# The list products of stage one moved into the slots of the masks

## The chip, the cores and the metric

The kernel runs on one core of a Trainium2 chip. The metric is the device time of one execution in microseconds; several executions are measured and their median is given. Five engines work side by side, each through its own instructions in order: TensorE (PE in the profile, with its weight loads as PEld), VectorE (DVE), ScalarE (ACT), GpSimd (POOL) and SyncE (SP), which here only starts DMAs. Engines wait for each other through semaphores.

## The reference

One layer on 4096 nodes with 512 features: attention over a sparse adjacency matrix, then a mixture of experts.

```python
x = x + gnn(layernorm(x), adj)
#   q, k, v = x @ Wq[h], x @ Wk[h], x @ Wv[h]            8 heads of 64
#   scores = q k^T / 8 + 0.01 eye - 1e16 (1 - max(adj, eye))
#   out = sum over h of softmax(scores) v @ Wo[h]
x = x + ffn(layernorm(x))
#   logits = x @ Wg + bg; the two best of 8 experts, softmax of their logits as weights
#   y_e = gelu(x @ W1[e] + b1[e]) @ W2[e] + b2[e]
```

The adjacency matrix is random and thin, denser for the first nodes than for the last.

## The kernel before, in words

Rows are handled in 32 tiles of 128 nodes, and eight groups of four tiles. The kernel has a stage one (projections and lists), a stage two (attention over lists of needed keys, with the routing of the experts beside it) and a stage for the experts. If a list has no room, a general path runs afterwards; it isn't used with this data.

**Stage one** (lines 322 to 623) does two things at once.

- *Projections.* For each of the 32 tiles x is normalised (`stats`, `norm` on VectorE), turned on TensorE (`turn_x`, two halves) and multiplied with the weights of k, v and, one block of four tiles later, q. Each product has four parts of 128 x 512 (lines 589 and 604). ScalarE copies the sums out of PSUM, and ScalarE's queue stores them to DRAM (`kv_d`, `q_d`).
- *Lists.* The adjacency matrix is loaded in 64 pieces, each of four row tiles by 512 columns, into seven buffers (`load_a`). `masks` (line 478) multiplies a piece with a small matrix `pw` of 32 columns, once for each of the four tiles, each into its own 32 partitions; so the array works in tiles of 128 rows by 32 columns. The result packs 16 rows into a number, and tells whether a column has an edge in the upper or lower half of a tile. ScalarE copies it, `turn_masks` turns it back on TensorE (line 492), ScalarE casts the words (line 496), and VectorE makes the indicators `ind` (line 497). When eight pieces of a group are done, `places` works out which list position each needed key gets: `classes`, `number` (two small products, lines 180 and 183), `ranks`, `outer`, `slots`, all else on VectorE. `group_lists` then builds the lists. `rows` and `values` fill `r_all` (lines 268, 277), one buffer that all groups share. `hot` (line 281) builds one of 16 one-hot matrices, in five buffers. `quads` (line 294) multiplies one of them: eight small products, 128 rows by 32 columns, into the four quarters of one PSUM tile; two `quads` make the sixteen that the profile shows together. `copy` takes the sum to SBUF on ScalarE, and `keys` turns it (line 308) and makes the indices `idx` on VectorE (lines 310 to 315).

The order is written out by hand. The function `job(n, f)` puts a piece of work into slot n; `step()` issues the work of the next slot in the order in which it was put there, and one part of a projection (two instructions of TensorE) follows it. There are 384 slots: eight for each of the first four tiles, twelve for each other, sixteen at the end. `masks(h)` stands in slot 5 + 5h, its turning three slots later. With s the slot behind the last mask of a group by five (s = 45 + 40g for group g), `places` takes the slots s, s+1, s+2, s+5 and s+8, and the jobs of `group_lists` follow. The masks of the following groups stand at s, s+5, s+10 and so on up to slot 320, so jobs of neighbouring groups are interleaved.

**Stage two** starts by closing the buffers of stage one. One large tile, `ring`, takes the place of most of them; SP loads a tile's own rows and its q (lines 691, 709), and POOL gathers the keys and values of the lists into it (line 696). TensorE turns the keys (line 723), ScalarE copies them (`kT`, line 725), and scores (line 760), exponentials (line 767), masks (line 773) and value products (line 788) follow.

Of the kernel before, what the change touches and what calls it, by code (L numbers as in the profile page):

```python
# [70 lines left out]
def fast(tc, dram, flag, x, adj, Wks, Wqs, Wvs, Wo, Wg, bg, W1, b1, W2, b2, out):  # L71
    with ExitStack() as ctx:
        _fast(ctx, tc, dram, flag, x, adj, Wks, Wqs, Wvs, Wo, Wg, bg, W1, b1, W2, b2, out)


def _fast(ctx, tc, dram, flag, x, adj, Wks, Wqs, Wvs, Wo, Wg, bg, W1, b1, W2, b2, out):
# [248 lines left out]
    with ExitStack() as s1:  # L325
# [198 lines left out]
        def job(n, f, *args):  # L524
            jobs.setdefault(n, []).append(lambda: f(*args))

        begins = [0]
        for i in range(NT):
            begins.append(begins[-1] + (2 * DC if i < TPB else 3 * DC))
            s = begins[i]  # L530
# [7 lines left out]
        for h in range(NHC):  # L538
            s = 5 + 5 * h
            job(s, masks, h)  # L540
            job(s + 1, load_a, h + 7)
            job(s + 3, turn_masks, h)
            g, c = divmod(h, NH)
            if c == NH - 1:
                s += 5
                hold = {}

                def ready(g=g, hold=hold):
                    hold["p"] = places(g, inds[g], lp, ps_l, "l")
                    hold["l"] = group_lists(g, rp, ohp, ps_l, "l")  # L550

                def call(hold, k, n, *args):
                    hold[k][n](*args)

                job(s, ready)
                for d, n in ((0, 0), (1, 1), (2, 2), (5, 3), (8, 4)):
                    job(s + d, call, hold, "p", n)
                job(s + 9, call, hold, "l", 0)
                job(s + 10, call, hold, "l", 1)
                for x2 in range(NT // 2):  # L560
                    job(s + 11 + 2 * x2, call, hold, "l", 2, x2)
                    job(s + 16 + x2 // 2 * 4, call, hold, "l", 3, x2)
                job(s + 44, call, hold, "l", 4)
                job(s + 47, call, hold, "l", 5)

        def extras():
            nc.scalar.dma_start(out=wg, in_=Wg.rearrange("(c p) e -> p c e", p=P))
# [1425 lines left out]
```

## Time and profile before

| | us |
|---|---|
| median of 3 runs | 2074.48 (2071.14 to 2076.76) |
| the profiled execution | 2230.39 |
| its span | 2228.6 |
| stage one: first and last projection product | 7.6 to 465.56 |
| TensorE busy, whole span | 2003.9 (90%) |
| VectorE busy, whole span | 959.3 (43%) |
| ScalarE busy, whole span | 790.9 (35%) |
| list products, line 294 | 1024 instructions, 26.9 busy |
| mask products, line 478 | 256 instructions, 26.1 busy |
| projection products, lines 589 and 604 | 768 instructions, 387.6 busy |

A line of the profile gives the source line, the engine, the operation, what is written and read with sizes, and how often. In the order of time, the first two numbers are the start and the time that the line covers, and the bracket tells how long the engine was idle before and what released it. In the table of stretches, each engine's busy time stands with its number of instructions, followed by the granted TensorE clock, the share of the DMA engines' time and GB/s. In the list of waits, the numbers are the total time, how often, and the longest. The profiled execution is longer than the runs without a profile.

### The profile page before, as it was taken

How to read it: one execution, taken by the hardware profiler on the slowest of the kernel's cores; microseconds unless marked ns; L12 is line 12 of the kernel's file. 1: busy time of each engine (PE TensorE's matmuls, PEld its weight loads, DVE VectorE, ACT ScalarE, POOL GpSimd, SP SyncE). 2: the span in 40 equal slices, each digit the busy share in tenths (PEclk: the TensorE clock that was granted, in tenths of full speed). 3: DMA queues.
4: the chain of work that ended last, by engine and by line, in shares of the span. 5: the costliest groups of instructions: out<-in, count | busy, mean ns of one | idle time of the engine just before them, and what ended most of it. 6: DMA issues, size and time to landing. Idle time of an engine off the chain costs nothing. (4 is left out here: it accounts for less than half of the span.)

```text
span 2228.6 us, 59742 instructions
## 1 busy us (share of the span) xinstructions
PE 2003.9 (90%) x25491; PEld 1329.7 (60%) x25491; DVE 959.3 (43%) x2501; ACT 790.9 (35%) x1152; POOL 611.7 (27%) x721
## 2 busy tenths in 40 slices
PE   9899999979999879888969697887967999999996
PEld 4344444459887757767858586776754444444443
DVE  3455655525444434534535344443554333333332
ACT  3232333235554534534535253443421222222221
POOL 2000000054444345433243443324122222222221
PEclk9999999989999979989989798998978999999998
DMA  9778775287777568767576575766686455565542
GB/s 371 253 251 257 255 246 179 77 350 252 246 259 257 201 228 266 249 206 239 190 267 232 202 255 204 255 201 222 227 278 195 104 115 113 111 144 111 110 72 44
DMA packets 193411, 462.01 MB, mean 207 GB/s; under 512 B 30384, under 2 KB 46768, under 8 KB 193008
## 3 DMA queue, kind: packets, MB, share of 16 engines
q0 software_dynamic: 67024, 249.44, 36.8%
q1 hardware_dynamic: 101808, 177.51, 24.8%
q10 hardware_dynamic: 24304, 31.11, 4.0%
q8 instruction: 206, 3.38, 0.6%
q14 instruction: 69, 0.57, 0.1%
HBM read 385.37 MB, written 72.64 MB: 206 GB/s over the span
## 5 line engine op out<-in xcount | busy, mean ns | idle before, releaser
L696 POOL DMA_INDIRECT ring<-kv_d,idx x361 | 407.3, 1128 | 978.1 <-ACT l L303 438.0
L760 PE MATMUL ps<-q,kT 64*64 64x64 f32 (+1 forms) x10224 | 356.5, 242 | 112.4 <-issue 96.0
L773 DVE SCALAR_TENSOR_TENSOR pr<-t,pr 128x1024 f32<-128x1024 uint16 x238 | 284.9, 1226 | 369.8 <-ACT pr L767 367.4
L760 PEld LDWEIGHTS ps<-q,kT 64*64 64x64 f32 (+1 forms) x10224 | 304.3, 151 | 166.1 <-issue 135.9
L788 PE MATMUL o<-ring,pr 128*64 128x65 f32 x8640 | 308.9, 228 | 31.6 <-issue 31.3
L725 ACT COPY kT<-pkT 128x512 f32<-128x512 f32 (+1 forms) x270 | 198.8, 783 | 375.5 <-PE pkT L723 268.6
L767 ACT ACTIVATE pr<-ps 128x1024 f32<-128x1024 f32 x270 | 271.4, 1025 | 139.4 <-PE ps L760 104.0
L788 PEld LDWEIGHTS o<-ring,pr 128*64 128x64 f32 x8640 | 282.1, 141 | 52.3 <-issue 37.5
L1341 PE MATMUL ph<-ring,xT 128*128 (+1 forms) x528 | 238.2, 594 | 0.8 <-ACT xT L1303 0.8
L723 PE MATMUL pkT<-ident,ring 128*128 128x128 f32 x1572 | 211.3, 282 | 18.3 <-issue 16.7
L723 PEld LDWEIGHTS pkT<-ident,ring 128*128 128x128 f32 x1572 | 180.0, 145 | 46.3 <-issue 38.7
L1392 POOL DMA_INDIRECT out_dram<-y,r x66 | 101.8, 1542 | 366.2 <-ACT y L1387 266.8
L1370 PE MATMUL py_e<-ring,hT 128*128 (+1 forms) x396 | 182.3, 596 | 1.6 <-ACT hT L1363 1.6
L1341 PEld LDWEIGHTS ph<-ring,xT 128*128 128x128 f32 (+1 forms) x528 | 91.3, 183 | 99.8 <-issue 98.7
L1387 ACT ACTIVATE y<-y,wt 128x512 f32<-128x512 f32 x66 | 47.6, 722 | 269.6 <-DVE y L1383 229.8
L604 PE MATMUL pv<-wv,xT 128*128 128x512 f32 x256 | 131.3, 608 | 0.0
L604 PE MATMUL pk<-wk,xT 128*128 128x512 f32 x256 | 130.4, 621 | 0.7 <-ACT xT L399 0.7
L589 PE MATMUL pq<-xT,wq 128*128 128x512 f32 x256 | 125.9, 607 | 0.0
L1029 POOL DMA_INDIRECT xs_d<-x,slot_i x64 | 64.6, 1010 | 203.2 <-DVE t L735 90.2
L828 PE MATMUL py<-wo,oT 128*128 128x512 f32 x256 | 119.3, 609 | 0.7 <-ACT oT L822 0.7
L1346 DVE COPY h<-ph 128x512 f32<-128x512 f32 x66 | 45.6, 692 | 169.6 <-PE ph L1341 166.1
L1370 PEld LDWEIGHTS py_e<-ring,hT 128*128 128x128 f32 (+1 forms) x396 | 67.2, 183 | 76.0 <-issue 74.1
(293 smaller groups left out, 1893.7 us busy)
## 6 DMA issues: line engine op xcount, KB each, us to landing
adj<-in_adj_dram SPq DMA_DIRECT2D x64, 1024.0 KB
wo<-in_L_ffn_W_dram SPq DMA_DIRECT2D x72, 256.0 KB
kv_d<-kvr ACTq DMA_DIRECT2D x32, 516.0 KB
ring<-kv_d SPq DMA_DIRECT2D x32, 516.0 KB
r<-xs_d SPq DMA_DIRECT2D x57, 258.0 KB
ring<-in_L_ffn_W_dram SPq DMA_DIRECT2D x56, 256.0 KB
xt<-in_x_dram SPq DMA_DIRECT2D x32, 256.0 KB
q_d<-qT ACTq DMA_DIRECT2D x32, 256.0 KB
```

The source lines that it names most:

```text
L589: nc.tensor.matmul(pq, w["q"][:, c, ts(p, P)], xTs[b][:, c, :], start=(c == 0), stop=(c == DC - 1),)
L604: nc.tensor.matmul(pk, xTs[b][:, c, ts(t, P)], w[n][:, c, :], start=(c == 0), stop=(c == DC - 1),)
L696: nc.gpsimd.indirect_dma_start(out=g, out_offset=None, in_=kv_d, in_offset=bass.IndirectOffsetOnAxis(ap=idx[i // GL][:, i % GL, a : a + 1] ...
L723: nc.tensor.transpose(pk[:, x * NP + p, :], g[:, ts(p, P)], ident)
L725: nc.scalar.copy(kT[:, : nk * NP], pk[:, : nk * NP])
L760: nc.tensor.matmul(ps[c : c + nk, r, p * P + x * nq : p * P + (x + 1) * nq], kT[r * KD : (r + 1) * KD, p, c : c + nk], q[r * KD : (r + 1) ...
L767: nc.scalar.activation(pr.rearrange("p h q -> p (h q)"), ps.rearrange("p r f -> p (r f)"), AF.Exp)
L773: nc.vector.scalar_tensor_tensor(pr, st["t"].unsqueeze(1).to_broadcast([P, H, P]), 0.0, pr, op0=ALU.is_gt, op1=ALU.mult,)
L788: nc.tensor.matmul(o[c * HALF : (c + 1) * HALF, h // NP, (h % NP) * VW : (h % NP + 1) * VW], pr[:, hd * NP + p, c * HALF : (c + 1) * HALF] ...
L828: nc.tensor.matmul(hold["py"], hold["oT"][:, c, :], wo[:, c, :], start=(c == 0), stop=(c == NP - 1),)
L1341: nc.tensor.matmul(ph[a], xTs[b][:, c, a], w, start=(c == 0), stop=(c == DC - 1), skip_group_check=b >= FULL,)
L1370: nc.tensor.matmul(py[a], hTs[b][:, c, a], w, start=(c == 0), stop=(c == HC - 1), skip_group_check=b >= FULL,)
```

## The change

The jobs of `group_lists` get other slots. `rows` and `values` move one slot back, from s+9 and s+10 to s+10 and s+11. The one-hot matrices were built every second slot from s+11; now two are built in every five slots, at s+10, s+12, s+15, s+17 and so on to s+47. The products of two one-hot matrices stood together every fourth slot from s+16 to s+44; now they stand every fifth slot from s+15 to s+50, which are the slots of the following groups' masks. `copy` and `keys` go from s+44 and s+47 to s+52 and s+55. `places` and the masks keep their slots. Within a slot, a group's list jobs are put in before the masks of the groups behind it.

```diff
                 for d, n in ((0, 0), (1, 1), (2, 2), (5, 3), (8, 4)):
                     job(s + d, call, hold, "p", n)
-                job(s + 9, call, hold, "l", 0)
-                job(s + 10, call, hold, "l", 1)
+                job(s + 10, call, hold, "l", 0)
+                job(s + 11, call, hold, "l", 1)
                 for x2 in range(NT // 2):
-                    job(s + 11 + 2 * x2, call, hold, "l", 2, x2)
-                    job(s + 16 + x2 // 2 * 4, call, hold, "l", 3, x2)
-                job(s + 44, call, hold, "l", 4)
-                job(s + 47, call, hold, "l", 5)
+                    m = 5 * (x2 // 2)
+                    job(s + 10 + m + 2 * (x2 % 2), call, hold, "l", 2, x2)
+                    job(s + 15 + m, call, hold, "l", 3, x2)
+                job(s + 52, call, hold, "l", 4)
+                job(s + 55, call, hold, "l", 5)
```

The numbers behind "l" are the places in the list that `group_lists` returns: 0 `rows`, 1 `values`, 2 `hot`, 3 `quads`, 4 `copy`, 5 `keys`.

## The prediction

> **What bounds the kernel now.** I read the page first, then the busy time by stretch, then the costliest groups of the first 470 us, the waits, and last the order of time. Slots are those of the code: one slot is one `step()` and the projection product behind it, 384 in all, slot 0 near 7.6 us, the last product ending at 465.56. Busy time of PE, PEld, DVE, ACT, POOL by stretch:
>
> ```profile
> 100.00:150.00 50.00, 50.00 (x299) 22.71 (x300) 28.90 (x86) 16.43 (x36) 0.00 (x0) 1.00 0.74 246
> 150.00:200.00 50.00, 50.00 (x309) 22.21 (x307) 27.55 (x83) 16.10 (x37) 0.00 (x0) 1.00 0.78 252
> 250.00:300.00 50.00, 50.00 (x309) 22.79 (x297) 27.25 (x84) 16.26 (x36) 0.00 (x0) 1.00 0.76 254
> ```
>
> In stage one TensorE has no free moment at full clock (1.00), VectorE is busy 55%, the DMA engines 0.74 to 0.78. Stage one ends when TensorE ends, so time taken out of TensorE's stream is won, unless VectorE becomes late. From the waits of this stretch:
>
> ```profile
> DVE oh L281 <- PE list L294: 12.7, 5, 2.9
> PEld L294 <- DVE oh L281: 3.0, 4, 0.8
> PEld L478 <- DMA adj<-in_adj_dram: 2.3, 3, 0.8
> ```
>
> The mask products wait little for the adjacency loads (2.3 us in all). The second line is the weight loader's idle time; whether the list products are delayed is seen in the order of time, which also gives the prices (start, us, engine):
>
> ```profile
> 156.05 1.02 PE L604 MATMUL pk<-wk,xT 128*128 128x512 f32 x2
> 157.00 0.42 PE L294 MATMUL list<-oh,r_all 128*32 128x128 f16 x16
> 157.35 1.13 PE L604 MATMUL pk<-wk,xT 128*128 128x512 f32 x2
> 158.31 0.60 PE L492 MATMUL pwt<-ident,ws 128*128 128x128 f32 x4
> 158.75 1.88 PE L604 MATMUL pk<-wk,xT 128*128 128x512 f32 x4
> 160.56 0.41 PE L478 MATMUL pwd<-adj,pw 128*32 128x512 bf16 x4
> 160.90 1.13 PE L604 MATMUL pv<-wv,xT 128*128 128x512 f32 x2
> ...
> 165.87 1.02 PE L589 MATMUL pq<-xT,wq 128*128 128x512 f32 x2
> 166.82 0.42 PE L294 MATMUL list<-oh,r_all 128*32 128x128 f16 x16
> 167.06 0.41 PE L478 MATMUL pwd<-adj,pw 128*32 128x512 bf16 x4
> 167.40 1.13 PE L589 MATMUL pq<-xT,wq 128*128 128x512 f32 x2
> ```
>
> A projection product is two instructions, 0.429 us from start to start (1.88 us for four is three such steps and 0.59). List products alone: 157.35 - 156.05 = 1.30, less 2 x 0.429 = 0.44, and the product behind them starts its second half 0.11 late (1.13 against 1.02): 0.55 us. Mask products alone: 160.90 - 158.75 = 2.15, less 4 x 0.429 = 0.43, plus 0.11: 0.54. Both in one slot: 167.40 - 165.87 = 1.53, less 0.86, plus 0.11: 0.78. I took the same difference over all of stage one: 31 list products alone 0.543 to 0.552, 44 mask products alone 0.535 to 0.538, 9 pairs 0.770 to 0.785. So a pair costs 0.547 + 0.537 - 0.777 = 0.307 us less than its two parts, and no list product is late now (none above 0.552).
>
> **What the skill says.** The Trainium skill, "TensorEngine Tiling (Array Packing)", Key Properties: "Changing tiling mode (not just tile) drains the TensorE". The trace agrees: in front of each such stretch the step is 0.52 instead of 0.43, and behind it the next weights are loaded in the open (0.11). "TensorE: Matmul & The Clock Gate", Part 2, says that weight loads are pulled ahead of running matmuls; the table shows that this is lost at a change. "Perfetto Trace Analysis", Tensor Engine Instruction: TensorE's ends are modelled, and VectorE and ScalarE run strictly in order. So I use starts, and treat VectorE as a queue.
>
> **The change part by part.** Nothing is added or removed: each group still has 16 `hot`, 16 `quads`, and one each of `rows`, `values`, `copy`, `keys`. No DMA is issued by a moved job.
>
> *Pairs.* Group g ends at s = 45 + 40g, and masks stand at multiples of 5, the last at slot 320. Before, quads stand at s+16, 20, 24 ... 44, so only s+20 and s+40 meet a mask: 13 pairs (two each for g = 0 to 5, one for g = 6). After, they stand at s+15, 20 ... 50: eight pairs each for g = 0 to 5, five for g = 6, none for g = 7: 53. In such a slot quads come first and masks directly behind, as in the 13. That is 40 new pairs x 0.307 = 12.3 us won. Lost: seven list products stood beside a mask's turning, which saved 0.04 to 0.05 each: 0.3. Net 12.0.
>
> *VectorE's order.* Before, a group's last two one-hots (s+39, s+41) are built ahead of the next group's `ranks`; after, they stand at s+45 and s+47, behind `ranks` and between it, `outer` and `slots`. In exchange `keys` leaves that place (s+47 to s+55). From the order of time around 166 to 187: `ranks` takes 168.72 to 172.34 = 3.62, `outer` 173.87 to 177.03 = 3.16, `slots` 178.96 to 180.74 = 1.78, a one-hot 0.61, statistics 0.84, normalising 0.65, an `ind` 0.1. With t = 0 at the first scan, one-hot 15 ends at 3.62 + 0.1 + 0.61 + 3.16 + 0.84 + 0.61 + 0.13 = 9.1; 9.7 where normalising stands there too. TensorE reaches its quads (s+50) after N 0.33, nine slots 7.72, two turnings 0.88, a pair 0.78 and one or two halves of x's turning 0.2 to 0.4, less 0.36 from N's start to the scan: 9.6 to 9.8. The margin, about 2 us or more before, is half a microsecond to nothing.
>
> *The wait that is new.* `rows` of the next group (s+50) overwrites `r_all`, which quads 14 and 15 of the same slot read; before, five slots lay between. Behind it on VectorE are values and the first one-hots, for which the quads of s+55 wait. But VectorE comes to `rows` only at about 9.1 + 1.78 + 0.75 = 11.6, and TensorE has left those quads by 10.1, so it costs nothing; if VectorE were early it would wait, harmlessly, for 1.5 us. From 11.6, rows, values (0.99 and 0.88 at twelve columns) and two one-hots end at 14.8; TensorE comes to s+55 at 9.7 + 0.78 + 4.29 + 0.44 + 0.2 = 15.4. For group 0 `rows` and `values` take 2.0 each; its one-hots are ready 1.7 us ahead now and its quads move 1.4 earlier (a slot and a mask). Going through all groups so, with the trace's durations and each engine in order, I get delays of 0.4 in three groups: 1.2 us. That walk, made for the order of before, hits the traced start of each VectorE block to 0.3 us where stage one runs undisturbed. Bounds: 0 and 1.5 us per group, 10.5.
>
> *The end of stage one.* The ring of stage two lies where `r_all` and the one-hots lay, so its first loads wait for the last quads:
>
> ```profile
> 451.96 0.42 PE L294 MATMUL list<-oh,r_all 128*32 128x128 f16 x16
> 452.43 0.63 SPq L709 DMA_DIRECT2D q<-q_d  x1
> 453.29 1.07 POOL L696 DMA_INDIRECT ring<-kv_d,idx  x1 [438.02 <-ACT l L303]
> ...
> 473.56 0.29 DVE L735 TENSOR_TENSOR t<-own_words,bits 128x128 uint16<-128x128 uint16 x1 [16.71 <-DMA q_d<-qT]
> 473.82 0.59 ACT L725 COPY kT<-pkT 128x512 f32<-128x512 f32 x1 [6.90 <-issue]
> ```
>
> These quads move from slot 369 to 375, six slots or 5.15 us nearer the end; SP's queue (q, own rows) and POOL's gathers start that much later against the end. The page names the copy of the list (slot 369, then 377), which is eight slots, 6.9. What hides it: stage two can't go on before 473.8, when the last q_d store, issued at 466.95, has landed. By the trace's landings gather 1 is there at 460.6, gathers 2 and 3 at 465.0, gather 4 at 466.5; TensorE needs them at 467, 468 and 474.5. Moved by 5 to 7 us, only 2 and 3 are late for their first use, and the store still sets the end. Later turns (483, 490) use gathers that landed 11 us and more before. I take 0; the other end is 5.2 us of loss where the cover is gone; a gain of 1.5 us is possible, since fewer gathers stand beside that store. The last keys (slot 380) are used near the end of stage two.
>
> **Sum.** 12.3 - 0.3 - 1.2 - 0 = 10.8 us off the profiled 2230.39 us (span 2228.6, 1.8 around it). The median of the runs shown, 2074.48, is 156 us lower; stage one's products already run at full clock, so I take the 10.8 unscaled: 2063.7 us, 0.5% faster. About 0.3% (6.2 us) is what a measurement can tell from no change.
>
> **Rivals.**
> - VectorE as the wait in place of the drain: 0.9 to 1.6 us of delay in each of seven groups eats 6 to 11 of the 12.0: 2069 to 2074, taken at 2072. For: margins near zero. Against: VectorE idles for 3 to 4 us between two `ind` in mid-group and catches up. Chance 0.13.
> - Stage two starts later: the 5.2 us not hidden: 2069. For: gathers keep the DMA engines full from 453. Against: the 473.8 above. Chance 0.10, half of it below the bound.
> - The adjacency loads are the limit and TensorE waits for them instead: 2074. Against: seven buffers and 0.76 of DMA time. Also here: the change does nothing, the pair's price holding only in the places seen. Chance 0.05.
> - Slower: the same VectorE queue between s+41 and s+55, but late by more than 12.0 / 7 = 1.7 us in each group, the point from which it decides. That needs 2 us more work or waiting in 15 us than the traced durations give, say where ScalarE holds `ind` behind a statistics wait in every group. At 3 us: 7 x 3 - 12 = 9 slower, 2083. Chance 0.06.
>
> **How the numbers follow.** Likeliest, 0.66: 2063.7, own range 2061 to 2067. Faster by over 0.3%: 0.66, half of the second rival and 0.06 of the first: 0.77. Same: 0.17. Slower: 0.06. The range runs from 2059.5 (no delays, 1.5 won at the stage's change, and the runs' scatter) to 2071, which takes in the second rival and part of the first and leaves out under 0.2.
>
> **What would show it.** Right: 53 pairs at 0.78 and 11 list products alone; the last projection product near 454.8 instead of 465.6; list products late by under 0.5 us, at x2 = 15 and x2 = 0 alone; first gather near 447.5; kT at 8 us behind the last product. Wrong: waits of list products for the one-hots of over 1 us in most groups; pairs above 0.9; more than 9 us from the last product to kT.

## The result and the profile after

| | before | after |
|---|---|---|
| median of the timed runs, us | 2074.48 (2071.14 to 2076.76) | 2068.03 (2065.06 to 2070.81) |
| ratio, 95% interval | | 0.9973 [0.9960, 0.9986] |
| stage one, from the start of the first product to 0.43 behind the start of the last, us | 457.85 | 447.83 |
| list and mask products sharing a stretch | 13 | 53 |
| list products alone | 51 | 11 |
| mask products alone | 51 | 11 |

The kernel became 6.45 us faster, 0.31% by the medians and 0.27% by the ratio of the runs, so just about what the prediction called measurable; 2063.7 was forecast, with a range to 2071. Stage one became 10.0 us shorter in the two profiled executions. So about 3.6 us of what was won in stage one did not arrive at the end.

One thing has to be known to read the profiles. The kernel before takes about 2223 us on two chips used below and 2074.77 on a third. By its time the profile of before (2230.39 us) comes from a chip like the first two; behind the end of stage one it is about 150 us longer than the profile of after (2070.29 us), which comes from one like the third, as the timed runs do. It is not the profiling that makes it longer: each profiled execution of the other kernels lies within the range of that kernel's timed runs (after: 2065.06 to 2070.81). So stage one is compared between these two profiles, stage two is not. For stage two the same kernels were run side by side on one chip, below.

Stretches of stage one in the kernel after; per engine the busy time and the number of instructions, then clock, DMA share and GB/s:

```profile
100.00:150.00 50.00, 50.00 (x319) 23.64 (x318) 29.25 (x86) 17.05 (x38) 0.00 (x0) 1.00 0.76 252
150.00:200.00 50.00, 49.88 (x318) 23.41 (x317) 29.56 (x88) 16.83 (x38) 0.00 (x0) 1.00 0.79 270
250.00:300.00 50.00, 50.00 (x321) 23.91 (x320) 29.41 (x88) 17.07 (x38) 0.00 (x0) 1.00 0.80 269
```

TensorE is as full as before and gets more done: 319, 318 and 321 instructions against 299, 309 and 309 in the same 50 us. VectorE rises with it to 58 or 59%, and the DMA engines to 0.76 to 0.80; neither has become the limit. The order of time on TensorE in the kernel after (start, us, instruction):

```profile
152.47 0.42 PE L294 MATMUL list<-oh,r_all 128*32 128x128 f16 x16
152.72 0.40 PE L478 MATMUL pwd<-adj,pw 128*32 128x512 bf16 x4
153.05 1.13 PE L590 MATMUL pq<-xT,wq 128*128 128x512 f32 x2
...
157.98 0.42 PE L294 MATMUL list<-oh,r_all 128*32 128x128 f16 x16
158.23 0.40 PE L478 MATMUL pwd<-adj,pw 128*32 128x512 bf16 x4
158.56 1.12 PE L605 MATMUL pv<-wv,xT 128*128 128x512 f32 x2
...
163.93 0.42 PE L294 MATMUL list<-oh,r_all 128*32 128x128 f16 x16
164.17 0.40 PE L478 MATMUL pwd<-adj,pw 128*32 128x512 bf16 x4
164.50 1.12 PE L590 MATMUL pq<-xT,wq 128*128 128x512 f32 x2
```

Lines behind line 565 have moved by one (L590 was L589). In these lines every list product has the mask product 0.24 or 0.25 us behind it, and one long product step (1.12 or 1.13 instead of 1.02) behind both: the open weight load is paid once. Read as in the prediction, the 39 plain pairs cost 0.775 us (median), 8 pairs with a turning of x beside them 0.997 (that turning alone costs 0.221), and 6 with the turning of a list 0.887 (0.112 alone). The waits of the kernel after (total, how often, longest):

```profile
DVE oh L281 <- PE list L294: 15.4, 5, 4.0
PEld L478 <- DMA adj<-in_adj_dram: 1.5, 2, 0.8
PE list L294 <- DVE oh L281: 0.7, 2, 0.4
PEld L294 <- DVE oh L281: 0.5, 1, 0.5
```

The mask products wait even less for the adjacency loads (1.5 us against 2.3). The last two lines are where TensorE waits for one-hots: the late list products of the prediction. The largest loss is at 223 us: the last list products of group 2, whose one-hots stand behind the places of group 3 on VectorE (L224 to L249). The second half of the stretch is 0.42 us late:

```profile
222.91 0.29 DVE L232 TENSOR_TENSOR place<-place,part 128x128 f32<-128x128 f32 x1
223.12 0.69 DVE L281 TENSOR_TENSOR oh<-sp,count 128x1024 f16<-128x1024 f16 x1
223.13 0.30 PE L294 MATMUL list<-oh,r_all 128*32 128x128 f16 x8
223.85 0.30 PE L294 MATMUL list<-oh,r_all 128*32 128x128 f16 x8 [0.42 <-DVE oh L281]
```

And the change of stage:

```profile
446.45 0.42 PE L294 MATMUL list<-oh,r_all 128*32 128x128 f16 x16
446.91 0.64 SPq L710 DMA_DIRECT2D q<-q_d  x1
447.77 1.07 POOL L697 DMA_INDIRECT ring<-kv_d,idx  x1 [432.46 <-PE list L294]
...
458.55 0.66 PE L724 MATMUL pkT<-ident,ring 128*128 128x128 f32 x4 [1.85 <-DMA ring<-kv_d,idx]
...
462.64 0.29 DVE L736 TENSOR_TENSOR t<-own_words,bits 128x128 uint16<-128x128 uint16 x1 [9.79 <-DMA q_d<-qT]
462.81 2.48 ACT L726 COPY kT<-pkT 128x512 f32<-128x512 f32 x4 [7.27 <-DMA q_d<-qT]
```

Stage one ends at 454.74. The last list product is 8.1 us ahead of that (13.2 before) and the first gather 7.0 (12.1 before). TensorE now waits for a gather at 458.55, but `kT` still waits for the store of q and starts 8.1 us behind the end, as it did before (8.4).

### The profile page after: what moved, and what is told of

The parts are those of the page before. It is cut to its first block, busy times and chain, and to the rows that moved or that the text cites. A ratio compares the mean times of both kernels' runs of the same rounds, so it can differ in the third digit from the quotient of the medians.

```text
span 2068.6 us, 59754 instructions
## 1 busy us (share of the span) xinstructions
PE 1927.7 (93%) x25491; PEld 1287.7 (62%) x25491; DVE 957.1 (46%) x2501; ACT 790.9 (38%) x1152; POOL 605.1 (29%) x721
## 5 line engine op out<-in xcount | busy, mean ns | idle before, releaser
L697 POOL DMA_INDIRECT ring<-kv_d,idx x361 | 395.5, 1096 | 840.7 <-PE list L294 432.5
L789 PE MATMUL o<-ring,pr 128*64 128x65 f32 x8640 | 297.5, 225 | 44.2 <-issue 44.0
L761 PE MATMUL ps<-q,kT 64*64 64x64 f32 (+1 forms) x10224 | 306.6, 237 | 31.1 <-issue 23.3
L761 PEld LDWEIGHTS ps<-q,kT 64*64 64x64 f32 (+1 forms) x10224 | 272.6, 148 | 64.1 <-issue 44.0
L789 PEld LDWEIGHTS o<-ring,pr 128*64 128x64 f32 x8640 | 273.1, 139 | 62.6 <-issue 47.3
L724 PE MATMUL pkT<-ident,ring 128*128 128x128 f32 x1572 | 204.7, 279 | 8.0 <-DMA ring<-kv_d,idx 2.8
L1342 PEld LDWEIGHTS ph<-ring,xT 128*128 128x128 f32 (+1 forms) x528 | 91.3, 183 | 99.8 <-issue 98.7
L605 PE MATMUL pk<-wk,xT 128*128 128x512 f32 x256 | 125.7, 610 | 0.7 <-ACT xT L399 0.7
L1030 POOL DMA_INDIRECT xs_d<-x,slot_i x64 | 69.8, 1090 | 186.1 <-DVE t L736 89.1
L590 PE MATMUL pq<-xT,wq 128*128 128x512 f32 x256 | 123.1, 603 | 0.0
```

Source lines behind the costliest of these rows:

```text
L590: nc.tensor.matmul(pq, w["q"][:, c, ts(p, P)], xTs[b][:, c, :], start=(c == 0), stop=(c == DC - 1),)
L605: nc.tensor.matmul(pk, xTs[b][:, c, ts(t, P)], w[n][:, c, :], start=(c == 0), stop=(c == DC - 1),)
L697: nc.gpsimd.indirect_dma_start(out=g, out_offset=None, in_=kv_d, in_offset=bass.IndirectOffsetOnAxis(ap=idx[i // GL][:, i % GL, a : a + 1] ...
L724: nc.tensor.transpose(pk[:, x * NP + p, :], g[:, ts(p, P)], ident)
L761: nc.tensor.matmul(ps[c : c + nk, r, p * P + x * nq : p * P + (x + 1) * nq], kT[r * KD : (r + 1) * KD, p, c : c + nk], q[r * KD : (r + 1) ...
L789: nc.tensor.matmul(o[c * HALF : (c + 1) * HALF, h // NP, (h % NP) * VW : (h % NP + 1) * VW], pr[:, hd * NP + p, c * HALF : (c + 1) * HALF] ...
```

## The experiments

My theory: a shared change of tiling saves 0.307 us, and what is won in stage one is lost in part because stage two's loads begin later against its end. The rivals: the pairs save less than their price says; or something else moves stage two. Three chips were used: on the first two the kernel before takes 2222.93 and 2222.78 us, so they are called the slow ones; the third is like that of the result (2074.77). "Stage one" is measured as in the table above, in the profiled execution, and "E" is its end.

**The pair by itself.** `apart` is the changed kernel with its list products one slot later, beside the masks and not with them; rows and values follow by a slot. All else, the late end too, stays.

```diff
-                job(s + 10, call, hold, "l", 0)
-                job(s + 11, call, hold, "l", 1)
+                job(s + 11, call, hold, "l", 0)
+                job(s + 12, call, hold, "l", 1)
...
-                    job(s + 15 + m, call, hold, "l", 3, x2)
+                    job(s + 16 + m, call, hold, "l", 3, x2)
```

> The changed kernel with every list product one slot later (s+16, s+21 ...), and rows and values one slot later with them: the same work in nearly the same order on VectorE, but no list product shares a slot with masks, so no pair is left of 53. If the change of tiling is the price (A and B): stage one 53 x 0.307 = 16.3 us longer than in the changed kernel, less 1.2 of delays that fall away, 15 us; 4.3 us longer than before; in all 2079 to 2083 us, ratio 1.002 to 1.004. If the gain came from something else in the new order: as the changed kernel, 2068.

Measured on the first chip: 2234.24 us, ratio to before 1.0046 [1.0033, 1.0060]; stage one 461.67. The changed kernel's stage one is 446.56 on the second chip, 447.83 in the profile above: 13.8 to 15.1 us less, where 53 pairs at 0.307, less the 1.2 of delays forecast, make 15.1. The order of time of this kernel shows the two apart:

```profile
155.30 0.41 PE L478 MATMUL pwd<-adj,pw 128*32 128x512 bf16 x4
155.64 1.12 PE L590 MATMUL pq<-xT,wq 128*128 128x512 f32 x2
156.70 0.41 PE L294 MATMUL list<-oh,r_all 128*32 128x128 f16 x16
157.04 1.98 PE L605 MATMUL pk<-wk,xT 128*128 128x512 f32 x4
```

Each stretch again has its own product step of 1.12 us behind it. So what was won in stage one is the shared slot, not the even spacing by five. The total went up by 11.3 us against before, though stage one is only 3.65 longer than that of the kernel before on this chip (458.02): some 7 us were lost behind stage one. The late end can't be called the cause of all of it: `last_late`, next, has nearly the same late end and loses 1 to 3 us there.

**The end by itself.** `last_late` is the kernel before with the last group alone in the change's slots; no mask stands there, so no pair is made. `last_early` is the changed kernel with the last group's list products four slots apart, the last in slot 368 (before 369, after 375). `before_again` is the kernel before unchanged, to see what a build is worth.

`last_early`:

```diff
+                apart = 5 if g < NT // GL - 1 else 4
                 for x2 in range(NT // 2):
-                    m = 5 * (x2 // 2)
+                    m = apart * (x2 // 2)
...
-                job(s + 52, call, hold, "l", 4)
-                job(s + 55, call, hold, "l", 5)
+                job(s + 17 + 7 * apart, call, hold, "l", 4)
+                job(s + 20 + 7 * apart, call, hold, "l", 5)
```

`last_late`:

```diff
+                if g < NT // GL - 1:
+                    job(s + 9, call, hold, "l", 0)
...
+                else:
+                    job(s + 10, call, hold, "l", 0)
...
+                        m = 5 * (x2 // 2)
+                        job(s + 10 + m + 2 * (x2 % 2), call, hold, "l", 2, x2)
+                        job(s + 15 + m, call, hold, "l", 3, x2)
```

> The kernel before once more, for a profiled execution without the 156 us that the one shown had on top, and as a measure of the scatter. Both theories: ratio 1 within 0.15%, first to last projection product 457 us as before. They differ on the way from the last projection product to the first value product of stage two, which is 18 us in the changed kernel: if the later loads of stage two cost nothing (A), it is 17 to 19 us here too; if they eat 4 us of the gain (B), it is 13 to 15 us.

> The kernel before, but the last group alone in the slots of the change: no new pair, the last list product in slot 375. A: 2075 us, ratio 1.0003 (a delay of 0.7 us in stage one by the walk through the engines). B: 2079 us, ratio 1.002.

> The changed kernel, but the last group, which has no masks to pair with, keeps its list products four slots apart, so the last of them stands in slot 368 instead of 375 and the first loads of stage two may start 6 us earlier against the end of stage one. The pairs are the same 53. A (late loads cost nothing): as the changed kernel, 2068 us, ratio to before 0.997. B (they eat 4 us): 2064 us, ratio 0.995, and the way from the last product to the first value product 4 us shorter.

Measured on the first chip, where all three ran beside the same runs of before (2222.93): `before_again` 2224.9, ratio 1.0005 [0.9992, 1.0017]; `last_late` 2226.69, ratio 1.0020 [1.0008, 1.0031], stage one 459.06, 1.0 longer than `before_again`; `last_early` 2213.68, ratio 0.9957 [0.9942, 0.9971], stage one 446.56. The unchanged kernel, built anew, is within its interval of before, and its median 2.0 us above. The late end alone costs 3.8 us against the runs of before and 1.8 against that build, of which 1.0 lies in stage one. With pairs and an early end, 9.2 us against the runs of before arrive, where 11.5 were won in stage one.

The recorded sign, the way from the last projection product to the first value product, speaks for late loads costing nothing in `before_again` (18.7 us) and `last_early` (18.7, not 4 less), but with the late end it is 23.8 in `last_late` and 23.3 in `apart`. It scatters: in the profile of before, with an early end, it is 22.7, and on the second chip, below, 23.7 with the late end and 22.4 with the early one.

**Both again, and TensorE kept busy.** In `last_late` and `apart` the clock of TensorE stood at half for 13.7 and 19.0 us up to the fifth block of exponentials of stage two, in `before_again` and `last_early` for 6.8. The Trainium skill, "TensorE: Matmul & The Clock Gate", Part 1, says that TensorE drops to half clock after an idle window. The traces agree in the long wait of stage one (in `last_late` TensorE is idle for 8.66 us up to 70.86, and at half clock from 66.1); in stage two half clock also followed 3.4 us in which TensorE was busy for 1.31 (`last_late`, from 472.3). So I gave TensorE transposes of the identity, of no use to the result, where it waits: 14 and 18 behind the second and third turning of keys in the changed kernel (`warm_late`), 46 behind the third in the one with an early end (`warm_early`). With them ran the changed kernel and `last_early` once more.

```diff
+        fill = []
...
+            for k in range({1: 14, 2: 18}.get(s, 0)):
+                if k == 0 and not fill:
+                    fill.append(ps_o.tile([P, 2, 512], F32, tag="o", name="fill"))
+                nc.tensor.transpose(fill[0][:, 0, ts(k % 4, P)], ident, ident)
```

(`warm_late`; in `warm_early` the numbers are `{2: 46}`.)

> The changed kernel once more, on the same chip as the three beside it. Stage one 447 to 448 us, 10 us shorter than before. B (late loads of stage two cost 3 to 6 us): 4 to 7 us faster than before, and 3 to 5 us slower than the same kernel with the last group's list products four slots apart. If that cost was an accident of the runs: 10 us faster than before, and level with it.

> The changed kernel with the last group's list products four slots apart. B: 9 to 11 us faster than before. If the cost of late loads was an accident: 10 us too; the difference to the changed kernel in the same runs decides, 3 to 5 us under B, under 1.5 us otherwise.

> The changed kernel, with 14 and 18 idle products of the identity on TensorE (1.5 and 2 us at 0.109 each) behind the turning of the second and third step of stage two, where TensorE waits for gathers and for the last q store. If late loads cost mainly by TensorE's clock falling to half after such gaps (C): the half-clock stretches in the first 60 us of stage two fall away, and it is 3 to 5 us faster than the changed kernel. If they cost by later data alone (D): no gain, or 1 us slower.

> The kernel with the last group's list products four slots apart, and 46 idle products (5 us) behind the turning of the third step, where TensorE waited 6.1 us. C: the half-clock stretch of 7 us goes, 3 us faster than without them. D: level.

Measured on the second chip (before 2222.78):

| | us | ratio to before | stage one |
|---|---|---|---|
| after_again | 2220.66 | 0.9986 [0.9973, 1.0000] | 446.56 |
| last_early_again | 2209.74 | 0.9939 [0.9918, 0.9960] | 447.33 |
| warm_late | 2234.25 | 1.0051 [1.0037, 1.0065] | 448.36 |
| warm_early | 2230.56 | 1.0029 [1.0016, 1.0043] | 447.06 |

The early end is 10.9 us faster here, with a stage one that is not shorter. A part of it is seen in the first 30 us behind E and the 56 us after those. The kernel after on the second chip:

```profile
454.00:484.00 30.00, 19.57 (x283) 16.23 (x282) 7.09 (x16) 11.34 (x14) 19.84 (x20) 0.77 1.03 413
484.00:540.00 56.00, 54.23 (x1083) 49.84 (x1085) 27.88 (x41) 29.72 (x39) 23.61 (x23) 0.94 0.85 289
```

The same stretches, from its own E, with the early end:

```profile
454.70:484.70 30.00, 20.71 (x355) 18.22 (x356) 8.55 (x18) 13.48 (x16) 14.84 (x16) 0.77 1.03 414
484.70:540.70 56.00, 53.70 (x1120) 49.22 (x1118) 29.25 (x45) 30.77 (x41) 25.27 (x23) 1.00 0.85 278
```

355 products of stage two done against 283 in the first 30 us, by DMA engines that are full in both (1.03, 413 and 414 GB/s). The fifth block of exponentials, counted from none, starts 31.7 us behind E with the late end and 27.4 with the early one (26.0 in `before_again`, 23.7 in `last_early`, 28.0 in the profile of before, 32.6 in `apart`, 31.7 in `last_late`); the twenty-ninth 98.2 against 92.8. On chips as slow as these, the four profiles with a late end have the twenty-ninth at 98.2 to 99.0, the five with an early one at 89.8 to 93.6. So about 5 us or more are lost by then with a late end. What becomes of them later differs: `last_late` is 8.3 us behind `before_again` at the twenty-ninth block (98.7 and 90.4) and 2.4 at the end; here 5.4 become 10.9 in the runs. In the kernel with the late end, single copies and products start late around 467 although no operand is missing by the trace:

```profile
466.89 0.94 POOL L697 DMA_INDIRECT ring<-kv_d,idx  x1 [0.99 <-DMA ring<-kv_d,idx]
...
466.92 0.59 ACT L726 COPY kT<-pkT 128x512 f32<-128x512 f32 x1 [3.39 <-remote]
...
468.30 0.27 PE L761 MATMUL ps<-q,kT 64*128 64x128 f32 x1 [1.31 <-issue]
```

What holds them isn't visible in the profile ("remote", "issue"). The clock doesn't explain the lateness at the fifth block: in `last_early_again` it stood at half for 13.7 us up to the fifth block, hardly less than the 14.9 of `after_again`; and with the fillers that time fell to 6.8 and 3.4 us, but the fifth block still came at 32.0 with the late end (26.5 with the early one), and the totals rose by 13.6 and 20.8 us. Both totals were against what either theory had forecast (3 to 5 us faster, or level to 1 us slower). In the profile of `warm_early`, against that of `last_early_again`, the time goes far from the fillers: the sixty-first block of exponentials is 1.1 us ahead, the 181st 14.3 behind. For `warm_late` no place is shown, since the profile of `after_again` is its slowest run (2228.81). I could not explain this at that point.

**On a chip like that of the result.** Four kernels: the changed one, the one with the early end, one with a still earlier end, and one that only has more instructions on TensorE. `last_soon` takes the last group's one-hots four at a time, its last list product in slot 361. `shift32` has 32 transposes of the identity in group 0, in slot 46, where TensorE waits for about nine microseconds in any case.

```diff
 last_soon (the last group alone)
+                        m = 6 * (x2 // 4)
+                        job(s + 12 + m + x2 % 4, call, hold, "l", 2, x2)
+                        job(s + 18 + m, call, hold, "l", 3, x2)
...
+                job(s + (38 if final else 52), call, hold, "l", 4)
+                job(s + (41 if final else 55), call, hold, "l", 5)
 shift32
         def number():
...
+            if g == 0:
+                for k in range(32):
+                    nc.tensor.transpose(
+                        pre.rearrange("p t c b -> p (t c b)")[:, ts(k % 3, P)], ident, ident
+                    )
```

> The changed kernel once more, as the measure of the other three. Stage one 446 to 448 us from first to last product; first gather of stage two 7 us ahead of the end of stage one; about 2 to 4 us faster than the kernel before, as in the last runs on such a chip.

> The changed kernel with the last group's list products four slots apart, so that the last stand in slot 368. Stage two's loads can begin 13 us ahead of the end of stage one instead of 7. If the late loads are the cost: 4 to 11 us faster than the changed kernel in the same runs, stage one level within 1 us. If the earlier difference was chance between builds: within 2 us.

> The changed kernel with the last group's list products behind every fourth one-hot instead of every second, the last in slot 361, and its copy and keys 14 slots earlier. Four turnings of the tiling fewer (4 stretches instead of 8, each turning 0.33 us by the trace), so stage one 1.2 us shorter than with the last in slot 368. The loads could begin 19 us ahead of the end of stage one by the list products, but then the store of the last tile's keys and values, landing about 14.6 us ahead, holds them. If the late loads are the cost: 1 to 3 us faster than with slot 368. If the loads have a threshold that slot 368 already meets: 1 us faster, from the turnings alone. If the loads don't matter: 1 us faster than the changed kernel.

> The changed kernel with 32 more transposes of the identity on TensorE in group 0, at slot 46, where TensorE waits 10 us for ScalarE and VectorE in any case; their results are not used. If what comes ahead of stage two in TensorE's stream moves stage two's time by itself, so that the fillers of the earlier runs cost for that reason: 8 us or more away from the changed kernel, with stage one level. If not: within 2 us of it, and the fillers' cost lay in their place.

Measured (before 2074.77; the last column is the start of the twenty-ninth block of exponentials behind E):

| | us | ratio to before | stage one | E to there |
|---|---|---|---|---|
| after_third | 2068.39 | 0.9965 [0.9952, 0.9978] | 447.65 | 87.8 |
| last_early_third | 2069.89 | 0.9978 [0.9964, 0.9993] | 446.34 | 86.6 |
| last_soon | 2064.67 | 0.9956 [0.9939, 0.9973] | 447.05 | 86.1 |
| shift32 | 2079.24 | 1.0021 [1.0005, 1.0036] | 446.96 | 88.2 |

The change again is 6.4 us faster than before by the medians. The early end, expected 4 to 11 us faster, is not faster here at all: a miss. Its expectation named this result, level within 2 us, as the sign that the earlier difference was chance between builds. Up to the twenty-ninth block it is ahead by 1.2 us, and `last_soon` by 1.7, one profile each, and no more is seen of a cost of the late loads there; the fifth block comes at 22.8, 22.7 and 22.0, the first value product 18.1 us behind the last projection product with the late end and 18.0 with the early one. `last_soon`'s four stretches in the other tiling fewer showed as worked out (47.64 to 46.38 us from slot 335 to E). It is the fastest of all, but it isn't told apart from the changed kernel, 3.7 us above it: their intervals overlap.

`shift32` decides the other question. The transposes are hidden in the wait, as this stretch of its order of time shows:

```profile
60.31 3.66 PE L182 MATMUL pre<-ident 128*128 128x128 f32 x32
71.27 0.48 PE L185 MATMUL tot<-cls,ones 128*128 128x384 bf16 x1 [7.30 <-DVE cls L175]
```

In the changed kernel on the same chip the same product waits without them:

```profile
71.02 0.48 PE L180 MATMUL tot<-cls,ones 128*128 128x384 bf16 x1 [8.80 <-DVE cls L175]
```

Stage one is level (446.96 and 447.65), and the total is 10.9 us longer, by the medians of 22 runs each. Where the time goes, the profiles don't show. That of `shift32` is of its fastest run (2071.19) and takes 1615.1 us behind E; the changed kernel takes 1607.6 in `after_third` and 1613.8 in the profile of the result, and the runs of `after_third` lie between 2060.70 and 2077.99. So two executions of one kernel differ by as much. The same stretch of stage two in these three, `after_third` first, then the profile of the result, then `shift32`:

```profile
957.50:1122.50 165.00, 154.36 (x3446) 131.97 (x3442) 84.69 (x212) 83.93 (x104) 77.39 (x83) 0.98 0.79 275
957.50:1122.50 165.00, 153.83 (x3516) 132.05 (x3510) 86.14 (x213) 85.62 (x105) 75.53 (x84) 0.99 0.78 272
957.50:1122.50 165.00, 151.51 (x3370) 129.05 (x3360) 82.00 (x203) 83.33 (x103) 74.73 (x81) 0.97 0.77 265
```

`shift32` has done 76 products fewer here than `after_third`, but the profile of the result, with the same kernel as `after_third`, 70 more. So an edit that costs nothing where it stands moved the whole by 10.9 us, with no line of the profile that names a place or a cause. That fits the fillers' 13.6 and 20.8 us, which I had put to their place; whether theirs is the same effect wasn't tried apart. It also means that the totals of `apart` and of the early ends on the slow chips can't be put down to the late end alone; what is shown of the late end is the lateness up to the twenty-ninth block. What the effect is (where instructions lie in memory, how they are fetched, the phase of the gathers against TensorE) stays open.

## Why the prediction was right, and where it was off

- **Pairs: 40 x 0.307 = 12.3.** Right. 53 pairs and 11 list products alone were counted as forecast, the plain pair at 0.775 against 0.777. `apart` gives 13.8 to 15.1 us for undoing all 53 pairs.
- **What the skill says of the change of tiling.** The Trainium skill, "TensorEngine Tiling (Array Packing)", Key Properties, says that a change of mode drains TensorE; the trace agrees in both kernels: one product step of 1.12 or 1.13 us instead of 1.02 for each stretch, one fewer wherever two stretches became one. The size had to come from the trace.
- **VectorE: delays of 1.2 in three groups.** About right: four groups were late, not three. The list products at 176, 223, 316 and 406 us cost 0.30, 0.61, 0.31 and 0.43 more than their kind, 1.65 in all (2.2 in `after_again`); each time they are the last two of a group, behind the places of the next, as forecast. Waits under 0.15 us are not in the list of waits above, so it shows less. From slot 100 to slot 335, the even part of stage one, the kernel after takes 271.0 us (`after_again` 271.9), `before_again` 280.5: 8.6 to 9.5 won. By the forecast, pairs less delays there are 33 x 0.307 - 1.2 = 8.9. TensorE was not quite without a free moment, as the prediction had it from the stretches that it showed: near 220 us it waited 2.0 us for ScalarE in the profile of before, 1.2 in `before_again`, and 1.1 after.
- **No DMA limit, no wait on `r_all` of size.** Right: 1.5 us at the mask products, and none of list products for `rows`.
- **Slots at the end: last product near 454.8, first gather near 447.5, kT 8 us behind the last product's end.** Right to 0.5 us: last product at 454.31, first gather at 447.77, kT at 8.1.
- **"I take 0" for the later loads.** This is the step that was off. It looked at the start of kT and at the first uses of single gathers, few of which are late and those covered by the wait for q, and both came as said. But the gathers keep the DMA engines full for at least 30 us behind E, so a queue that starts 6 us later does not catch up: the twentieth gather lands 33.7 us behind E in `after_third`, 28.0 in `last_early_third`. Uses after the first few can meet that. On the slow chips this cost about 5 us up to the fifth block of exponentials; on the chip like that of the result 1.2 to 1.7 us up to the twenty-ninth. The other bound of the prediction, 5.2, is near what the slow chips show up to there. That the queue is what makes these blocks late fits the landings, but no run changed the queue alone.
- **The sum: 10.8.** Stage one gave 10.0 in the profiles of the two kernels, and 6.45 arrived. Of the missing 3.6, the late loads may be 1.2 to 1.7. The other 2 us have no shown cause: nothing in the sum allowed for the rest of the kernel moving by itself, and `shift32` shows that it does, by 10.9 us, for an edit with no cost of its own. Profiles of the kernel before on such a chip would be needed to place them; there are none. The total is outside the range that was held likeliest (2061 to 2067) and inside the one to 2071, which was drawn wide for the loss of 5.2 us of the second rival; that it also held what nobody had forecast is luck.

Of the rivals, "stage two starts later" is seen up to the twenty-ninth block on the slow chips and is at most a part of the truth on the other; VectorE as the limit, the adjacency loads, and the slower case did not happen.

## What to carry to other kernels

Where small products in another tiling stand singly between large ones, put those that can wait into one slot: the price of a pair, read from starts in the order of time, held for 40 more pairs to within 1% in the median. When a stage is made shorter, look at what the next one prefetches: the first transfers of a queue that starts later can still be in time and the tenth or twentieth be late, if the queue is full. And a difference of a few microseconds in a long stage that the edit doesn't touch isn't yet a reason: give the kernel an edit that costs nothing and see how far that moves it, and compare two profiles of one kernel before you read a difference between two kernels.

## What was not expected of the hardware

- 32 transposes hidden in a wait at 60 us made the kernel 10.9 us slower, with stage one level.
- The same kernel took 2074.77 us on one chip and 2222.78 on another, 7% more, with stage one within 1% (447.65 and 446.56 for the changed one): nearly all of the difference lies in stage two (the last block of exponentials starts 1175.0 us behind E in `after_again` and 1021.3 in `after_third`), and TensorE's half-clock time in the whole execution is 239 us against 103.
- What an edit is worth differs between such chips too: the early end brought 10.9 us on the second and nothing measurable on the third.
- Keeping TensorE busy with fillers while it waited took away half-clock time there (14.9 to 6.8 us and 13.7 to 3.4) and did not make that part of the kernel faster.
